# A graph layer's first stage: weights in one array, and layernorm chunks in a written order

## The chip, the core and the metric

The kernel runs on one core of a Trainium2 chip. The time is that of one execution on the device in microseconds (us); the median of several runs counts. A core has five engines that run side by side: PE (TensorE, matrix products), DVE (VectorE), ACT (ScalarE), POOL (GpSimd) and SP (SyncE, here only a sender of DMAs). Each takes its own instructions in order and waits for the others through semaphores. DMAs are sent from the queues of SP, ACT and POOL and are carried out by 16 shared DMA engines.

## What is computed

A graph network over 12,500 nodes of 64 values and 412,500 edges of 32 values, sorted by receiver:

```python
h = jnp.maximum(_layernorm(x, axis=-1), 0.0)
msg_in = concat(h[src], h[dst], edge_attr)
messages = swish(msg_in @ W1 + b1) @ W2 + b2
att = softmax(swish(msg_in @ Wa1 + ba1) @ Wa2 + ba2, axis=0)
aggregated = segment_sum(messages * att, dst, 12500)
out = x + swish(concat(h, aggregated) @ Wu1 + bu1) @ Wu2 + bu2
```

All of it is in 32-bit floats.

## The kernel before, in words

Nodes are padded to NB = 98 blocks of 128. Since `msg_in @ W` is a sum of a sender's, a receiver's and an edge's part, the kernel computes the first two once per node. The work has three stages.

**First stage** (lines 97 to 252). The weights are sent to SBUF by many small DMAs, 23 of the first DMAs on the ACT queue among them (with base_sb and the zeros behind tr_d), four on SP's. Some are laid out twice, so that one matrix product serves two blocks (`w_pair`, `we`), which needs memsets on DVE and several DMAs each; DVE then halves them, because swish is computed with tanh. x is read in seven chunks of 14 blocks (CB = 14), with three buffers `xc`. For each chunk DVE forms the mean (L208, L209), subtracts it (L211), ACT squares (L213), DVE sums the squares and scales (L215, L216), ACT takes the root (L217), DVE forms reciprocal and h (L218, L220). PE transposes h (L228), ACT copies the result to hT (L229), PE multiplies it by the sender weights (L234), ACT copies the product to ts (L236), and SP stores ts to ts_d in HBM (L237). Behind the chunks, ACT sends the store of hT (L238), DVE prepares the window numbers (`windows()`, L192 to L202), and a second loop makes the receivers' table: PE (L248), DVE adds the bias (L250), the ACT queue stores tr_d (L252), with two buffers `tr`.

The order of the instructions on each engine is set by a scheduler, from the dependences and its own costs, except where an instruction stands in `tc.keep_in_program_order` (named `pin` elsewhere): these keep the order in which they are written. In the first stage of the kernel before only the matmuls of the tr loop (L248) are so held.

**The loop over edges** (`one_pass`). For each of 403 groups of 1,024 edges POOL sends eight gathers (L373), each of 128 rows of ts_d by the indices in src_sb. There are eight buffers `gs`, so POOL may be eight groups ahead of those who read them. SP loads a window of tr_d, the edges' values and the receivers (`wins`, `eo`, `db`), PE multiplies (L400), DVE adds the gathered rows (L405), and ACT, DVE and PE work on the result. Before the loop DVE makes constants (L315 to L337), among them `wu2h`, loaded by two DMAs of the ACT queue (L326) and halved (L327). The memory of these constants and of `eo` and `db` is that of the first stage, set free when its last stores have landed.

**The update** at the end reads the sums and writes the output.

A DMA from SP or ACT takes one of eight semaphore lanes in turn. The instruction that sends it also waits for the DMA that had that lane eight transfers earlier.

Of the kernel before, what the change touches and what calls it, by code (L numbers as in the profile page):

```python
# [51 lines left out]
P = 128  # L52
# [18 lines left out]
BIG = 3.0e38  # L71
WHY = "a receiver's number; windows past the last node are padded"
# [3 lines left out]
def gnn_kernel(ctx: ExitStack, tc: tile.TileContext, n_edges, x, src, dst, dst_row, first, edge,  # L76
               W1, b1, W2, b2, Wa1, ba1, Wa2, ba2, Wu1, bu1, Wu2, bu2, out):
# [5 lines left out]
    CB = 14 if NB % 14 == 0 else 1  # L83
# [17 lines left out]
    w_pair = const.tile([P, 2, 2, C], F32, name="w_pair")  # L101
    nc.vector.memset(w_pair, 0.0)
    for r in range(2):
        for h, eng in ((0, nc.sync), (1, nc.scalar)):
            rows = slice(h * D, (h + 1) * D)
            eng.dma_start(w_pair[rows, r, h, 0:U], Wa1[r * D:(r + 1) * D, :])
            eng.dma_start(w_pair[rows, r, h, U:C], W1[r * D:(r + 1) * D, :])
    w_bu = const.tile([D + 1, U], F32, name="w_bu")
    nc.scalar.dma_start(w_bu[:D, :], Wu1[0:D, :])
    nc.scalar.dma_start(w_bu[D:D + 1, :], bu1[None, :])  # L110

    we = const.tile([P, C], F32, name="we")
    nc.vector.memset(we, 0.0)
    for r in (0, 64, 96):
        nc.scalar.dma_start(we[r:r + DE, 0:U], Wa1[2 * D:, :])
        nc.scalar.dma_start(we[r:r + DE, U:], W1[2 * D:, :])
    nc.vector.tensor_scalar(we, we, 0.5, None, op0=ALU.mult)
# [3 lines left out]
    nc.scalar.dma_start(base_sb[:, :NG], first)  # L121

    def across(ap, n, name, dtype=F32, parts=P):
        t = const.tile([parts, n], dtype, name=name)
        nc.scalar.dma_start(t, bass.AP(tensor=ap.tensor, offset=ap.offset, ap=[[0, parts], [1, n]]))
        return t

    bias = const.tile([P, C], F32, name="bias")
    for ap, c in ((ba1, 0), (b1, U)):
        nc.scalar.dma_start(bias[:, c:c + U],  # L130
                            bass.AP(tensor=ap.tensor, offset=ap.offset, ap=[[0, P], [1, U]]))
    wa2 = across(Wa2, U, "wa2")
    ba2_c = across(ba2, 1, "ba2_c")
    bu2_r = across(bu2, D, "bu2_r")
    w2b = const.tile([S1, U], F32, name="w2b")
    nc.scalar.dma_start(w2b[:U, :], W2)
    nc.scalar.dma_start(w2b[U:S1, :], b2[None, :])
    wu1a = const.tile([U, U], F32, name="wu1a")
    nc.scalar.dma_start(wu1a, Wu1[D:, :])
    wu2 = const.tile([U, D], F32, name="wu2")  # L140
    nc.scalar.dma_start(wu2, Wu2)
# [19 lines left out]
    nc.scalar.dma_start(tr_d[NP:, :], zero[:WR, :])  # L161
# [11 lines left out]
    with tc.tile_pool(name="node1", bufs=1) as node1, \  # L173
            tc.tile_pool(name="node", bufs=2) as node, \
            tc.tile_pool(name="node_ps", bufs=2, space=PSUM) as node_ps:
        x_v = x.rearrange("(p b) d -> p b d", b=NB)
        xcs = []
        for c in range(0, NB, CB):
            xc = node.tile([P, CB, D], F32, name="xc", bufs=3)
            nc.sync.dma_start(xc, x_v[:, c:c + CB, :])  # L180
            xcs.append(xc)
        nc.sync.dma_start(src_sb, src)
        dst_sb = node1.tile([P, T], I32, name="dst_sb")
        nc.sync.dma_start(dst_sb, dst)
        base_p = node1.tile([P, NG], I32, name="base_p")
        nc.sync.dma_start(base_p, bass.AP(tensor=first.tensor, offset=first.offset,
                                          ap=[[0, P], [1, NG]]))
        hT = node1.tile([2 * D, NB // 2, P], F32, name="hT")

        def windows():  # L190

            nc.vector.tensor_tensor(dloc.rearrange("p (g k) -> p g k", k=K),  # L192
                                    dst_sb.rearrange("p (g k) -> p g k", k=K),
                                    base_p[:, :, None].to_broadcast([P, NG, K]), ALU.subtract)
            last4 = dloc.rearrange("p (g k) -> p g k", k=K)[:, :, H:]
            nc.vector.tensor_scalar(last4, last4, -float(SHIFT), None, op0=ALU.add)
            for h in range(2):
                nc.vector.tensor_scalar(bj[:, :, h], base_p[:WR, :], iota_p[:WR], float(SHIFT * h),
                                        op0=ALU.add, op1=ALU.add)
            fall = node1.tile([P, NG - 1], F32, name="fall")  # L200
            nc.vector.tensor_tensor(fall, base_p[:, :NG - 1], base_p[:, 1:], ALU.subtract)
            nc.vector.tensor_reduce(far[:, 2:3], fall, AX.X, ALU.max)  # L202

        nc.vector.tensor_scalar(w_pair, w_pair, 0.5, None, op0=ALU.mult)
        for c in range(0, NB, CB):
            xc = xcs[c // CB]
            mean = node.tile([P, CB], F32, name="mean")
            nc.vector.tensor_reduce(mean, xc, AX.X, ALU.add)  # L208
            nc.vector.tensor_scalar(mean, mean, 1.0 / D, None, op0=ALU.mult)  # L209
            xm = node.tile([P, CB, D], F32, name="xm")  # L210
            nc.vector.tensor_tensor(xm, xc, mean[:, :, None].to_broadcast([P, CB, D]), ALU.subtract)  # L211
            sq = node.tile([P, CB, D], F32, name="sq")
            nc.scalar.activation(sq, xm, AF.Square)  # L213
            rstd = node.tile([P, CB], F32, name="rstd")
            nc.vector.tensor_reduce(rstd, sq, AX.X, ALU.add)  # L215
            nc.vector.tensor_scalar(rstd, rstd, 1.0 / D, EPS, op0=ALU.mult, op1=ALU.add)  # L216
            nc.scalar.activation(rstd, rstd, AF.Sqrt)  # L217
            nc.vector.reciprocal(rstd, rstd)  # L218
            h = node.tile([P, CB, D], F32, name="h")
            nc.vector.scalar_tensor_tensor(h, xm, 0.0, rstd[:, :, None].to_broadcast([P, CB, D]),  # L220
                                           op0=ALU.max, op1=ALU.mult)
            ts = node.tile([P, CB, C], F32, name="ts")
            for b in range(0, CB, 8):
                n = min(8, CB - b)
                q = (c + b) // 2
                pt = node_ps.tile([P, 4, P], F32, name="pt")
                for i in range(n // 2):
                    nc.tensor.transpose(pt[:, i, :], h[:, b + 2 * i:b + 2 * i + 2, :], ident)  # L228
                nc.scalar.copy(hT[:, q:q + n // 2, :], pt[:, :n // 2, :])  # L229
                for i in range(0, n, 4):  # L230
                    m = min(4, n - i)
                    pn = node_ps.tile([P, 4, C], F32, name="pn", bufs=3)
                    for k in range(0, m, 2):
                        nc.tensor.matmul(pn[:, k:k + 2, :], hT[:, q + (i + k) // 2, :], w_pair[:, 0],  # L234
                                         start=True, stop=True)
                    nc.scalar.copy(ts[:, b + i:b + i + m, :], pn[:, :m, :])  # L236
            nc.sync.dma_start(ts_d.rearrange("(p b) f -> p b f", b=NB)[:, c:c + CB, :], ts)  # L237
        nc.scalar.dma_start(hT_d, hT)  # L238
        nc.vector.tensor_scalar(bias, bias, 0.5, None, op0=ALU.mult)
        windows()  # L240
        for c in range(0, NB, CB):
            tr = node.tile([P, CB, C], F32, name="tr")
            for b in range(0, CB, 4):
                n = min(4, CB - b)
                pn = node_ps.tile([P, 4, C], F32, name="pn", bufs=3)
                for i in range(0, n, 2):
                    tc.keep_in_program_order(
                        nc.tensor.matmul(pn[:, i:i + 2, :], hT[:, (c + b + i) // 2, :], w_pair[:, 1],  # L248
                                         start=True, stop=True))
                nc.vector.tensor_tensor(tr[:, b:b + n, :], pn[:, :n, :],  # L250
                                        bias[:, None, :].to_broadcast([P, n, C]), ALU.add)
            nc.scalar.dma_start(tr_d[:NP, :].rearrange("(p b) f -> p b f", b=NB)[:, c:c + CB, :], tr)  # L252
# [40 lines left out]
def one_pass(tc, n_edges, v):  # L293
# [6 lines left out]
    wa2, ba2_c, w2b, wu1a, wu2, we, gather = (  # L300
        v[k] for k in ("wa2", "ba2_c", "w2b", "wu1a", "wu2", "we", "gather"))
# [8 lines left out]
    with ExitStack() as ctx:  # L310
# [11 lines left out]

        wu2h = keep.tile([P, 2, D], F32, name="wu2h")
        nc.vector.memset(wu2h, 0.0)
        for h in range(2):
            nc.scalar.dma_start(wu2h[h * U:(h + 1) * U, h, :], wu2)  # L326
        nc.vector.tensor_scalar(wu2h, wu2h, 0.5, None, op0=ALU.mult)  # L327
# [486 lines left out]

# [38 lines left out]
```

## Time and profile before

| what | us |
|---|---|
| median of 3 runs | 4180.05 (4179.7 to 4185.37) |
| profiled execution | 4179.44 |
| its span, first to last instruction | 4177.7 |

Work of the first stage, from the groups between 20 and 98 us by shape:

| line, engine | shape | count | mean ns |
|---|---|---|---|
| L213 ACT square | 128x896 | 7 | 948 |
| L229 ACT copy to hT | 128x512 | 7 | 586 |
| L236 ACT copy to ts | 128x512 | 21 | 586 |
| L211 DVE subtract | 128x896 | 5 | 1072 |
| L215 DVE sum of squares | 128x896 | 7 | 1080 |
| L220 DVE h | 128x896 | 7 | 1087 |
| L192 DVE window numbers | 128x3224 | 1 | 3501 |

The profile is read as follows. A group's row names the line, the engine, the operation and its tiles with their shapes, then the busy time and the mean of one instruction, and behind a bar the engine's idle time just before such instructions with what ended it. "issue" there is time in which the engine waited for nothing that the profile shows. A row of the waits has the total, the number and the longest. In the timeline each row has the start and the duration in us; "SPq" and "ACTq" rows are the sending of DMAs, not the transfers. Trace records name two PE instructions for each 128x256 matmul in 32-bit floats, so "x14" are the seven products of a chunk.

### The profile page before, as it was taken

To read this page: it belongs to the slowest core of one execution; us is meant where nothing else is said; L and a number is where in the kernel's file an instruction comes from. 1 tells how busy PE (TensorE), PEld (TensorE's weight loads), DVE (VectorE), ACT (ScalarE), POOL (GpSimd) and SP (SyncE) were. 2 spreads that over 40 slices of the span, in tenths; PEclk is the share of its full clock that TensorE was granted. 3 is DMA by queue.
4 is the path that set the end of the run, shared out by engine and by line. 5 is a ranking of instruction groups with operands and counts; after the bars stand their busy time and mean duration, and the time that the engine had idled before them with its cause. 6 is when DMAs were issued, how large, how long until landed. Compare 5 with 4: busy or idle time off the path is not lost.

```text
span 4177.7 us, 43813 instructions
## 1 busy us (share of the span) xinstructions
PE 2250.2 (54%) x10980; PEld 1686.0 (40%) x10980; DVE 2879.0 (69%) x7713; ACT 600.1 (14%) x1229; POOL 3048.7 (73%) x3236
## 2 busy tenths in 40 slices
PE   5644556445555555555555555555555555555555
PEld 4433344333334433444334443343444334434344
DVE  5766767666767766766666666676676666766668
ACT  3211111111111111111111111111111111111112
POOL 2777777777777777777777777777777777777772
PEclk9566666666666666656666566566565665666665
DMA  6433334333333333333333333333323333333323
GB/s 246 112 86 101 101 95 102 96 100 103 95 95 91 83 88 89 81 89 83 87 89 80 89 86 84 90 80 90 90 80 90 82 88 90 80 90 82 87 77 110
DMA packets 232283, 392.22 MB, mean 94 GB/s; under 512 B 99797, under 2 KB 158294, under 8 KB 218838
## 3 DMA queue, kind: packets, MB, share of 16 engines
q0 software_dynamic: 103168, 211.49, 19.0%
q1 hardware_dynamic: 125808, 167.82, 15.3%
q10 hardware_dynamic: 3046, 10.02, 0.6%
q8 instruction: 91, 1.49, 0.2%
q14 instruction: 170, 1.39, 0.1%
HBM read 363.29 MB, written 25.72 MB: 93 GB/s over the span
## 4 chain that ended last, share of the span: by engine, by line


## 5 line engine op out<-in xcount | busy, mean ns | idle before, releaser
L373 POOL DMA_INDIRECT gs<-ts_d,src_sb x3224 | 3047.1, 945 | 1055.2 <-issue 884.1
L400 PE MATMUL pe<-wins,eo 128*128 128x256 f32 x3224 | 1405.3, 612 | 1183.2 <-issue 1132.6
L400 PEld LDWEIGHTS pe<-wins,eo 128*128 128x128 f32 x3224 | 959.6, 312 | 1460.3 <-issue 1198.1
L405 DVE TENSOR_TENSOR gs<-pe,gs 128x1024 f32<-128x1024 f32 x403 | 492.0, 1221 | 1115.7 <-DMA gs<-ts_d,src_sb 1108.2
L406 ACT ACTIVATE pe<-gs 128x1024 f32<-128x1024 f32 x403 | 415.6, 1031 | 2777.4 <-DVE gs L405 2315.9
L468 DVE TENSOR_SCALAR wt<-iota_w,dloc,p 128x40 f32<-128x40 f32 x3224 | 726.1, 317 | 0.1
L474 PE MATMUL sp<-wt,acts 128*65 128x40 f32 x6448 | 586.0, 261 | 0.9 <-DVE wt L468 0.9
L474 PEld LDWEIGHTS sp<-wt,acts 128*65 128x65 f32 x6448 | 535.3, 173 | 27.0 <-DVE wt L468 1.0
L444 PE MATMUL mt<-ident,mx 128*128 128x128 f32 x103 | 48.4, 470 | 515.0 <-DVE sums L498 508.8
L416 DVE SCALAR_TENSOR_TENSOR acts<-pe,gs 128x512 f32<-128x512 f32 x403 | 272.0, 675 | 27.6 <-ACT pe L406 27.6
L424 DVE TENSOR_TENSOR pe<-pe,wa 128x512 f32<-128x512 f32 x403 | 281.6, 699 | 12.8
L422 DVE SCALAR_TENSOR_TENSOR pe<-pe,gs 128x512 f32<-128x512 f32 x403 | 280.6, 696 | 11.5 <-ACT pe L406 0.2
L427 DVE TENSOR_REDUCE lg<-pe 128x8 f32<-128x512 f32 x403 | 276.9, 687 | 10.4
L396 DVE TENSOR_SCALAR eo<-db,bj 64x256 f32<-64x256 int32 x806 | 274.1, 378 | 7.6
L485 PEld LDWEIGHTS mt<-ss,w2u 65*64 65x64 f32 x806 | 99.8, 175 | 396.4 <-issue 383.4
L485 PE MATMUL mt<-ss,w2u 65*64 65x40 f32 x806 | 150.8, 281 | 162.9 <-DVE gm L451 150.9
L444 PEld LDWEIGHTS mt<-ident,mx 128*128 128x128 f32 x103 | 18.6, 180 | 528.2 <-DVE sums L498 521.1
L455 ACT ACTIVATE scale<-fall 128x1 f32<-128x1 f32 x103 | 20.9, 203 | 514.2 <-DVE fall L454 514.2
L499 DVE COPY sums<-nmax 64x40 f32 x403 | 79.6, 198 | 9.1 <-issue 0.3
L480 ACT COPY ss<-sp 65x40 f32<-65x40 f32 x403 | 73.4, 182 | 25.5 <-PE sp L474 25.3
L498 DVE TENSOR_TENSOR sums<-sums,mt 64x40 f32 x300 | 53.5, 178 | 2.9 <-PE mt L485 1.6
L275 ACT COPY bu<-mt 64x512 f32<-64x512 f32 x24 | 25.8, 1076 | 150.1 <-PE mt L272 144.4
(96 smaller groups left out, 596.7 us busy)
## 6 DMA issues: line engine op xcount, KB each, us to landing
gs<-ts_d,src_sb POOLq DMA_INDIRECT x3224
eo<-in_edge_dram SPq DMA_DIRECT2D x100, 512.0 KB
db<-in_dst_row_dram SPq DMA_DIRECT2D x200, 256.0 KB
wins<-tr_d SPq DMA_DIRECT2D x806, 32.0 KB
ts_d<-ts SPq DMA_DIRECT2D x7, 896.0 KB
tr_d<-tr ACTq DMA_DIRECT2D x7, 896.0 KB
xc<-in_x_dram SPq DMA_DIRECT2D x7, 448.0 KB
hT_d<-hT ACTq DMA_DIRECT2D x1, 3136.0 KB
```

The lines of the kernel that those rows point to most:

```text
L373: nc.gpsimd.indirect_dma_start(out=gs[:, j, :], out_offset=None, in_=ts_d[:, :], in_offset=bass.IndirectOffsetOnAxis(ap=src_sb[:, t + j:t ...
L396: pin(nc.vector.tensor_scalar(eo[:WR, e], db[:, e], bj[:, g, h:h + 1], None, op0=ALU.is_equal))
L400: pin(nc.tensor.matmul(pe[:, 2 * q:2 * q + 2, :], eo[:, q * P:(q + 1) * P], win[:, q // 2, :, :], start=True, stop=True))
L405: pin(nc.vector.tensor_tensor(gss[g], pes[g], gss[g], ALU.add))
L406: pin(nc.scalar.activation(pes[g], gss[g], AF.Tanh))
L416: pin(nc.vector.scalar_tensor_tensor(acts[g % ACTS][:, :, 0:U], th[:, :, U:C], 1.0, gs[:, :, U:C], op0=ALU.add, op1=ALU.mult))
L422: pin(nc.vector.scalar_tensor_tensor(att, th[:, :, 0:U], 1.0, gs[:, :, 0:U], op0=ALU.add, op1=ALU.mult))
L424: pin(nc.vector.tensor_tensor(att, att, wa2[:, None, :].to_broadcast([P, K, U]), ALU.mult))
L427: pin(nc.vector.tensor_reduce(lgs[s][:, k:k + K], att, AX.X, ALU.add))
L468: pin(nc.vector.tensor_scalar(wt[:, j, :], iota_w[:, j // H, :], dloc[:, g * K + j:g * K + j + 1], p[:, k + j:k + j + 1], op0=ALU.is_equal ...
L474: pin(nc.tensor.matmul(sp, acts[g % ACTS][:, j, :], wt[:, j, :], start=j == 0, stop=j == K - 1))
L485: pin(nc.tensor.matmul(pp, w2u, sps.pop(g), start=True, stop=True))
```

## The change

All weights are laid out on the host in one array of 128 partitions by 1281 values, with zeros, doubled and repeated parts in place; two DMAs of the ACT queue bring it, and one DVE operation halves the first 896 columns (`w_pair`, `we`, `bias`, `wu2h`). x is read in eight chunks of 8, 14, 14, 14, 14, 14, 12 and 8 blocks with a buffer for each. The layernorm is split into `squares`, `deviation`, `normal` and `senders`, whose instructions are all held in the order written, which interleaves the chunks. The mean's scaling goes into the subtraction and the variance's scaling and eps into ACT's root. The transposes of a chunk all stand ahead of its products, and `pn` has four buffers. The load of base_sb goes to SP. The stores of the zeros and of hT, and windows(), stand behind the loop that makes tr.

```diff
-    CB = 14 if NB % 14 == 0 else 1
+    CB = 14 if NB % 14 == 0 else 2
...
-    w_pair = const.tile([P, 2, 2, C], F32, name="w_pair")
-    nc.vector.memset(w_pair, 0.0)
-    for r in range(2):
-        for h, eng in ((0, nc.sync), (1, nc.scalar)):
-            rows = slice(h * D, (h + 1) * D)
-            eng.dma_start(w_pair[rows, r, h, 0:U], Wa1[r * D:(r + 1) * D, :])
-            eng.dma_start(w_pair[rows, r, h, U:C], W1[r * D:(r + 1) * D, :])
...
+    nh = sum(n for _, n in PARTS[:HALVED])
+    nc.scalar.dma_start(w_all[:, :nh], weights[:, :nh])
+    nc.scalar.dma_start(w_all[:, nh:], weights[:, nh:])
...
-    nc.scalar.dma_start(tr_d[NP:, :], zero[:WR, :])
...
-        for c in range(0, NB, CB):
-            xc = node.tile([P, CB, D], F32, name="xc", bufs=3)
-            nc.sync.dma_start(xc, x_v[:, c:c + CB, :])
+        sizes = [8] + [min(CB, NB - 16 - c) for c in range(0, NB - 16, CB)] + [8] if NB > 16 else [NB]
+        chunks = [(sum(sizes[:i]), n) for i, n in enumerate(sizes)]
+        for c, n in chunks:
+            xc = node.tile([P, CB, D], F32, name="xc", bufs=min(len(chunks), 8))[:, :n, :]
+            nc.sync.dma_start(xc, x_v[:, c:c + n, :])
             xcs.append(xc)
         nc.sync.dma_start(src_sb, src)
+        nc.sync.dma_start(base_sb[:, :NG], first)
...
+        def squares(i):
+            n = chunks[i][1]
+            total = node.tile([P, CB], F32, name="total")[:, :n]
+            pin(nc.vector.tensor_reduce(total, xcs[i], AX.X, ALU.add))
+            xm = xms[i] = node.tile([P, CB, D], F32, name="xm", bufs=3)[:, :n, :]
+            pin(nc.vector.scalar_tensor_tensor(xm, total[:, :, None].to_broadcast([P, n, D]), -1.0 / D,
+                                               xcs[i], op0=ALU.mult, op1=ALU.add))
+            sq = sqs[i] = node.tile([P, CB, D], F32, name="sq", bufs=3)[:, :n, :]
+            pin(nc.scalar.activation(sq, xm, AF.Square))
+
+        def deviation(i):
+            n = chunks[i][1]
+            rstd = rstds[i] = node.tile([P, CB], F32, name="rstd")[:, :n]
+            pin(nc.vector.tensor_reduce(rstd, sqs.pop(i), AX.X, ALU.add))
+            pin(nc.scalar.activation(rstd, rstd, AF.Sqrt, bias=eps, scale=1.0 / D))
+
+        def normal(i):
+            n = chunks[i][1]
+            rstd = rstds.pop(i)
+            pin(nc.vector.reciprocal(rstd, rstd))
+            h = hs[i] = node.tile([P, CB, D], F32, name="h")[:, :n, :]
+            pin(nc.vector.scalar_tensor_tensor(h, xms.pop(i), 0.0,
+                                               rstd[:, :, None].to_broadcast([P, n, D]),
+                                               op0=ALU.max, op1=ALU.mult))
+
+        def senders(i):
+            c, nn = chunks[i]
+            h = hs.pop(i)
+            ts = node.tile([P, CB, C], F32, name="ts")[:, :nn, :]
+            pts = []
+            for b in range(0, nn, 8):
+                n = min(8, nn - b)
+                pt = node_ps.tile([P, 4, P], F32, name="pt")
+                for k in range(n // 2):
+                    pin(nc.tensor.transpose(pt[:, k, :], h[:, b + 2 * k:b + 2 * k + 2, :], ident))
...
+                pin(nc.scalar.copy(hT[:, q:q + n // 2, :], pt[:, :n // 2, :]))
+            for b in range(0, nn, 4):
+                m = min(4, nn - b)
+                pn = node_ps.tile([P, 4, C], F32, name="pn", bufs=4)
+                for k in range(0, m, 2):
+                    pin(nc.tensor.matmul(pn[:, k:k + 2, :], hT[:, (c + b + k) // 2, :],
+                                         w_pair[:, 0], start=True, stop=True))
+                pin(nc.scalar.copy(ts[:, b:b + m, :], pn[:, :m, :]))
+            pin(nc.sync.dma_start(ts_d.rearrange("(p b) f -> p b f", b=NB)[:, c:c + nn, :], ts))
...
-        nc.scalar.dma_start(hT_d, hT)
-        nc.vector.tensor_scalar(bias, bias, 0.5, None, op0=ALU.mult)
-        windows()
...
+        squares(0)
+        if len(chunks) > 1:
+            squares(1)
+        pin(nc.vector.tensor_scalar(w_all[:, :nh], w_all[:, :nh], 0.5, None, op0=ALU.mult))
+        for i in range(len(chunks)):
+            deviation(i)
+            if i:
+                senders(i - 1)
+            if i + 2 < len(chunks):
+                squares(i + 2)
+            normal(i)
+        senders(len(chunks) - 1)
+        for c, nn in chunks:
...
+            pin(nc.scalar.dma_start(
+                tr_d[:NP, :].rearrange("(p b) f -> p b f", b=NB)[:, c:c + nn, :], tr))
+        pin(nc.scalar.dma_start(tr_d[NP:, :], zero[:WR, :]))
+        pin(nc.scalar.dma_start(hT_d, hT))
         windows()
...
-        wu2h = keep.tile([P, 2, D], F32, name="wu2h")
-        nc.vector.memset(wu2h, 0.0)
-        for h in range(2):
-            nc.scalar.dma_start(wu2h[h * U:(h + 1) * U, h, :], wu2)
-        nc.vector.tensor_scalar(wu2h, wu2h, 0.5, None, op0=ALU.mult)
```

## The prediction

> **What bounds the kernel now.** I first read the page's busy shares and its groups. The chain of waits, which would come next, is empty for this profile, so the bound has to be found from the waits and the timeline.
>
> ```profile
> span 4177.7 us, 43813 instructions
> PE 2250.2 (54%) x10980; PEld 1686.0 (40%) x10980; DVE 2879.0 (69%) x7713; ACT 600.1 (14%) x1229; POOL 3048.7 (73%) x3236
> ...
> L373 POOL DMA_INDIRECT gs<-ts_d,src_sb x3224 | 3047.1, 945 | 1055.2 <-issue 884.1
> ...
> L405 DVE TENSOR_TENSOR gs<-pe,gs 128x1024 f32<-128x1024 f32 x403 | 492.0, 1221 | 1115.7 <-DMA gs<-ts_d,src_sb 1108.2
> ```
>
> POOL is busy 73% and DVE, the next, 69%. But POOL's idle time is nearly all "issue": time in which it waited for nothing. DVE's largest wait is the other way round, for the gathered rows. The view of POOL's own waits splits POOL's idle time:
>
> ```profile
> POOL gs L373 <- issue: 884.1, 2901, 0.3
> POOL gs L373 <- DMA tr_d<-tr: 72.9, 1, 72.9
> POOL gs L373 <- DMA gs<-ts_d,src_sb: 53.3, 175, 0.3
> POOL gs L373 <- DVE eo L396: 27.1, 89, 0.3
> ```
>
> Every one of these waits is 0.3 us, the normal distance between two gathers, but for one of 72.9 us ahead of the first. So POOL never stalls once it has begun. The tile view puts the first gather at 75.3 and the last at 4103.8: (4103.8 - 75.3) / 3223 = 1.250 us each. The span is then **75.35 (first stage) + 3224 x 1.250 (4029.4) + 73.0 (what follows the last gather)** = 4177.7. The change touches only the first term and, by what it hands on, perhaps the second.
>
> What ends the 72.9 us? The label names the store of tr, but the gather (L373) reads ts_d and src_sb, and the compiled order has it wait on the queue lanes of the seven ts stores and not on those of hT_d or tr. The timeline of the first stage (start, duration) shows how the last of them comes about:
>
> ```profile
> 20.30 0.55 ACTq L161 DMA_DIRECT2D tr_d<-zero  x1
> ...
> 20.88 1.28 ACT L213 ACT_TABLE_LOAD   x1 [20.88 <-DMA wu1a<-in_Wu_dram]
> ...
> 22.17 1.79 ACT L213 ACTIVATE sq<-xm 128x896 f32<-128x896 f32 x2
> ...
> 35.64 0.99 ACT L229 COPY hT<-pt 128x512 f32<-128x512 f32 x2
> 35.78 28.94 SPq L237 DMA_DIRECT2D ts_d<-ts  x7
> 36.30 2.89 PEld L234 LDWEIGHTS pn<-w_pair,hT 128*128 128x128 f32 x14 [1.04 <-ACT hT L229]
> 36.30 3.29 PE L234 MATMUL pn<-w_pair,hT 128*128 128x256 f32 x14 [0.81 <-ACT hT L229]
> ...
> 60.98 0.35 ACTq L238 DMA_DIRECT2D hT_d<-hT  x1
> ...
> 75.35 1.10 POOL L373 DMA_INDIRECT gs<-ts_d,src_sb  x1 [72.95 <-DMA tr_d<-tr]
> ```
>
> Three pieces: ACT does nothing until 20.88 because its queue is issuing 23 small DMAs, each waiting for an earlier one's lane; seven chunks then take until the last ts store at 64.4 (tile view), 6 us each; and that store needs 75.35 - 64.4 = 10.9 us to land, beside the 3136 KB of hT_d issued 3.4 us earlier.
>
> **The change, part by part.** All times are from the span's start; chunks are now 8, 14, 14, 14, 14, 14, 12, 8 blocks.
>
> *Weights (2 DMAs in place of 21 on ACT and 4 on SP; base_sb goes to SP, the zeros go last).* ACT is free at about 2 us (two issues of 0.6 from 0.82); its table load of 1.28 needs no data. Five DVE operations on weights go here (memsets, halvings), two more in the loop's preparation; one halving of 128x896 comes, by L204's 0.43 for 512 elements some 0.7 us. SP sends x at once instead of after its four weight pieces. The bytes grow to 655 KB (zeros included); x (3.2 MB), weights, src and dst (1.6 MB each) are 7.3 MB, at the 292 to 366 GB/s of the rows 12 to 28 us some 22 us, but x goes first: a 448 KB chunk takes 1.5 us at that rate and is needed every 5.6 us. Hidden, except for the first two chunks: in before the first landed at 4.31; I take 4.0 for the first (256 KB) and 6.5 for the second.
>
> *The first chunk.* DVE: sum and centre chunk 0 (0.69 each, as L427 and L416 for 512 elements): 5.4; chunk 1 (1.08 twice) 6.5 to 8.7; halving 9.4; variance sum 0: 10.1; chunk 2: 12.3; reciprocal 0.2 and h 0.68: 13.2; variance sum 1: 14.3. ACT: squares 0 and 1 until 9.7, second table load until 11.0, sqrt 0, square 2 until 13.3, sqrt 1 (it waits for DVE) until 14.6. Only then, in the written order, the copies of chunk 0: hT 0.6, four matmuls at 0.72 (the first chunk's pace in before, 5.07 us for seven; 3.29 later) and the last copy: 18.6. Square 3 and sqrt 2: **19.85**. Removed means, scale and eps operations (0.17 each) are DVE work that is not on this path.
>
> *A chunk in the steady order.* DVE per 14 blocks: 4 x 1.08 + 0.23 = 4.55 us. ACT's written order is sqrt, two hT copies, four ts copies, square of two chunks on, next sqrt. From the trace of before, hT copy to first matmul is 35.64 to 36.30 = 0.66, the last ts copy ends 3.75 after the first matmul; square 0.95, sqrt 0.22, handoffs 0.05: 0.66 + 3.75 + 0.95 + 0.22 + 0.05 = **5.63**. That exceeds DVE's 4.55, so the ACT-PE ring paces. In before, hT copies came at 35.64, 40.06, 45.95, 51.19, 55.58: 4.4 to 5.9 apart, so pinning by itself gains little; it is the late start that goes.
> From 19.85: chunks 1 and 2, 5.63 each: 31.1; chunk 3 (12-block square 0.83): 36.6; chunk 4 (8-block square 0.57): 41.85; chunk 5 with only sqrt: 46.5; chunk 6, three full copies, 0.66 + 1.17 + 2 x 0.86 + 0.59 = 4.14: 50.6; chunk 7: 0.66 + 1.17 + 0.86 + 0.59 = 3.28: **53.9**.
> Here a rule bears: the Trainium skill, TensorE: Matmul & The Clock Gate, Part 1, says the array runs at half clock until it has been busy for a window of about 3.4 us, and again after an idle one. The rows by stretch (length, busy time and count of each engine, then granted clock, DMA share, GB/s):
>
> ```profile
> 72.00:76.00 4.00, 0.55 (x3) 0.14 (x1) 0.46 (x1) 0.00 (x0) 0.65 (x1) 1.00 1.01 418
> 76.00:80.00 4.00, 3.72 (x11) 2.90 (x12) 2.48 (x6) 0.00 (x0) 3.09 (x4) 0.71 0.70 275
> ```
>
> After a PE gap of 3.74 us inside these rows the clock fell to 0.71; but before's matmuls kept their 3.29 us a chunk after gaps of 0.4 to 1.7 us. The new ring leaves PE gaps of about 1.3 us, so I charge the slow pace once (1.0 us, in the sum). Were gaps of that kind to keep it cold, 1.8 us a chunk for six would add 10.7 and the gain would be 7.
>
> *The last store.* 512 KB, and hT_d and tr_d's tail of zeros no longer go ahead of it. Bounds: 10.9 us as now; the nearest clean row is the last tr store, issued at 93.0 (tile view) and landed at 97.27, 4.3 us for 896 KB; less 384 KB at the 382 GB/s of that stretch (1.0 us) is **3.3**. I take 3.3, since the 10.9 fits the bytes: 3.2 MB of hT_d and two stores of 0.9 MB from 61 to 75 us are 5 MB in 14 us, at the 361 to 470 GB/s these rows show. Against small transfers stands the Trainium skill, DMA: Bandwidth & Descriptors, section Bandwidth, that transfers below 1 MiB waste the rate[...]. In before ACT's ts copies never waited for a store 4.4 to 6.6 us old, so the extra store is not on the path; I charge nothing for it. First gather: 53.9 + 0.1 + 3.3 = **57.3**.
>
> *What is handed on.* hT_d now goes behind all tr stores. DVE's preparation of the loop (L315 on) and SP's loop loads reuse that memory, so they now wait for hT_d's landing. Bytes after 54 us: tr 6.4 MB and hT 3.2 MB; in before the rows of 64 to 96 us average 340 GB/s, with up to 52 for gathers in it (64 KB each 1.25 us); at 290 net that is 33 us, and 2 to land: about 89, against 97.27. From there to the first addition of gathered rows (L405) before took until 111.03, 13.8 us, set by the loads of wins (PE waited 14.9 for them), so the 4.6 us wait on wu2h that goes was beside them; about 103. POOL may run eight groups ahead (8 buffers x 10 us): until 57.3 + 80 = 137. The first group is done some 5 us after its addition, at 108: **29 us of cover**, so POOL doesn't stall. Then DVE needs about 6 us a group against POOL's 10 and catches up as it did before. Moving windows() (6 us on DVE) behind the tr stage, base_sb to SP (one issue of 0.3) and wu2h out of the loop's preparation cost nothing under that cover. The 73.0 us at the end stay.
>
> **Sum**: 75.35 - 57.3 = 18.0 us less. The profiled execution is 4179.44 (span 4177.7 and 1.7 around it), the median 4180.05, 0.6 apart, so 4180.05 - 18 = **4162**. An uncertain step is worth its own microseconds and nothing is multiplied; changes under 0.2% (8.4 us) can't be told from none.
>
> **Rivals.**
> 1. *The ring overlaps better*, and PE alone paces at 4.41 (before's last three chunks): 18.6 + 5 x 4.41 + 4.14 + 3.28 + 3.4 = 51.5, gain 24: 4156. For it: hT copies 4.4 apart in before. Against: there no square stood between them, in the new order one does.
> 2. *The last store lands no faster*, since tr stores still start as it goes: 53.9 + 10.9 = 64.8, gain 10.5: 4169.5. Against: tr's first store has only 512 KB and comes later.
> 3. *It doesn't do what it says*: PE stays cold, or ts stores wait behind the src and dst loads: gain under 8.4; 4173.
> 4. *Slower*: hT_d last holds the loop's start so long that the eight buffers run out. It decides only once hT_d lands after about 118 us (89 + 29), and then costs a microsecond for each; to be slower by 8.4 it would have to land after 144, at a mean rate of 109 GB/s. Rates of 183 to 382 with gathers running speak against it. 4189.
>
> **Chances.** Forecast 0.72 (4156.5 to 4168), rival 1 0.10, rival 2 0.11, rival 3 0.05, rival 4 0.02. Faster: 0.93; same: 0.05; slower: 0.02. The range, 4153 to 4170, takes in rivals 1 and 2.
>
> **What would show it.** First gather at 57 (51 to 65); 3224 gathers still 1.250 apart with no wait over 0.4; hT copies of the 14-block chunks 5.6 apart; first square near 5.5; last ts store issued near 54 and 3 to 4 us from the gather; the loop's first memset near 89 and L405's first near 103. Wrong if a gather waits for DVE or ACT, or the chunk pace is that of DVE or loads.

## The result, and the profile after

The changed kernel takes 4167.01 us (median of 7 runs, 4165.77 to 4167.37), the kernel before 4180.05 (7 runs, 4179.4 to 4185.37). The ratio is 0.9966, its 95% interval 0.9954 to 0.9977: 13.0 us less, where 18.0 were forecast. The forecast's ratio, 0.9957, lies in that interval too; that the gain was smaller is read from the runs, none of which is under 4165.77, and from the traces. The profiled execution of the changed kernel took 4166.68 us, 1.8 more than its span. First the page: span, busy shares, and the rows of the gather and of the addition of gathered rows (now L382 and L414).

```profile
span 4164.9 us, 43769 instructions
...
PE 2237.8 (54%) x10980; PEld 1678.3 (40%) x10980; DVE 2873.2 (69%) x7698; ACT 600.9 (14%) x1230; POOL 3052.8 (73%) x3236
...
L382 POOL DMA_INDIRECT gs<-ts_d,src_sb x3224 | 3051.2, 946 | 1038.3 <-issue 930.2
...
L414 DVE TENSOR_TENSOR gs<-pe,gs 128x1024 f32<-128x1024 f32 x403 | 491.8, 1220 | 1116.6 <-DMA gs<-ts_d,src_sb 1103.8
```

Hardly anything shows here, for the change moves some tens of microseconds out of four thousand. One number is new: the gathers are busy 3051.2 us and not 3047.1. The view of POOL's own waits shows the other sign (total, number, longest):

```profile
POOL gs L382 <- issue: 930.2, 2876, 54.0
POOL gs L382 <- DMA gs<-ts_d,src_sb: 60.8, 193, 1.7
```

The 54.0 is the wait ahead of the first gather, 72.9 before. But the second row's longest was 0.3 before and is 1.7 now: POOL does stall after it has begun. The timeline of the first stage (start, duration, engine, and in brackets the idle time before) shows the part that went as meant:

```profile
1.75 1.28 ACT L203 ACT_TABLE_LOAD   x1 [1.75 <-PEq L878]
6.26 0.63 ACT L203 ACTIVATE sq<-xm 128x512 f32<-128x512 f32 x1 [3.23 <-DVE xm L200]
...
20.14 0.95 ACT L231 COPY hT<-pt 128x512 f32<-128x512 f32 x2
...
25.45 0.96 ACT L231 COPY hT<-pt 128x512 f32<-128x512 f32 x2
...
52.16 0.58 ACT L238 COPY ts<-pn 128x512 f32<-128x512 f32 x1 [0.23 <-PE pn L236]
52.77 0.32 SPq L239 DMA_DIRECT2D ts_d<-ts  x1
...
56.44 1.10 POOL L382 DMA_INDIRECT gs<-ts_d,src_sb  x1 [54.04 <-issue]
```

ACT begins at 1.75 in place of 20.88, chunks follow 5.3 us apart, the last ts store goes at 52.77, and the first gather starts 3.67 later, at 56.44: **18.9 us sooner** than the 75.35 of before. So the first stage gave more than the kernel gained. The last gather starts at 4090.97; (4090.97 - 56.44) / 3223 = 1.2518 us from one to the next, where before had 1.2499 by the same count. Times 3223 that is **6.1 us lost**. From the start of the last gather to the end both take 73.9. 18.9 - 6.1 = 12.8, the difference of the two spans.

Where do the 6.1 go? POOL's timeline, early in its run:

```profile
76.58 0.94 POOL L382 DMA_INDIRECT gs<-ts_d,src_sb  x1 [0.30 <-issue]
77.83 3.36 POOL L382 DMA_INDIRECT gs<-ts_d,src_sb  x1 [0.30 <-issue]
81.49 1.32 POOL L382 DMA_INDIRECT gs<-ts_d,src_sb  x1 [0.30 <-issue]
...
91.86 0.94 POOL L382 DMA_INDIRECT gs<-ts_d,src_sb  x1 [0.30 <-issue]
93.20 0.94 POOL L382 DMA_INDIRECT gs<-ts_d,src_sb  x1 [0.40 <-DMA gs<-ts_d,src_sb]
95.82 0.94 POOL L382 DMA_INDIRECT gs<-ts_d,src_sb  x1 [1.67 <-DMA gs<-ts_d,src_sb]
97.38 0.94 POOL L382 DMA_INDIRECT gs<-ts_d,src_sb  x1 [0.62 <-DMA gs<-ts_d,src_sb]
98.85 0.94 POOL L382 DMA_INDIRECT gs<-ts_d,src_sb  x1 [0.53 <-DMA gs<-ts_d,src_sb]
```

Two things, both where before had gathers of 0.94 us and waits of 0.3. Two gathers are themselves long, by 2.42 and 0.38 us: 2.8. And four wait for the rows of earlier gathers, 0.1 + 1.37 + 0.32 + 0.23 = 2.0 above the usual 0.30. That leaves 1.3 us spread over the rest of the loop, which is no more than that rest differs between kernels: counted against 1.25 us a gather, the gathers after 104 us lost from -1.0 to +0.9 us in the traces of before, this kernel and the four that follow. DVE's timeline over the same stretch:

```profile
76.86 3.50 DVE L178 TENSOR_TENSOR dloc<-dst_sb,base_p 128x3224 f32<-128x3224 int32 x1
...
80.98 1.03 DVE L182 TENSOR_SCALAR dloc<-dloc 128x1612 f32<-128x1612 f32 x1
...
91.00 0.06 DVE L330 MEMSET nmax<- 128x1 f32 x1 [7.23 <-DMA hT_d<-hT]
...
105.02 1.23 DVE L414 TENSOR_TENSOR gs<-pe,gs 128x1024 f32<-128x1024 f32 x1 [8.15 <-PE pe L409]
```

The long gathers lie beside the two long operations of windows(). In before these ran ahead of all gathers:

```profile
34.38 3.50 DVE L192 TENSOR_TENSOR dloc<-dst_sb,base_p 128x3224 f32<-128x3224 int32 x1
...
40.87 0.99 DVE L196 TENSOR_SCALAR dloc<-dloc 128x1612 f32<-128x1612 f32 x1
```

The 3.36 us gather starts 0.97 after the DVE operation and ends at 81.19, 0.83 after that ends at 80.36; the second ends at 82.81, 0.80 after its DVE operation. That is nearly a whole gather (0.94) after DVE is done: as if POOL had stood still in between. The waits for rows come just as the large store of hT, issued at 78.0, has landed (91.0) and the loop's first loads go out.

### The profile page after: what moved, and what is told of

Read it like the earlier page. It is cut to its first block, busy times and chain, and to the rows that moved or that the text cites. A ratio compares the mean times of both kernels' runs of the same rounds, so it can differ in the third digit from the quotient of the medians.

```text
span 4164.9 us, 43769 instructions
## 1 busy us (share of the span) xinstructions
PE 2237.8 (54%) x10980; PEld 1678.3 (40%) x10980; DVE 2873.2 (69%) x7698; ACT 600.9 (14%) x1230; POOL 3052.8 (73%) x3236
## 4 chain that ended last, share of the span: by engine, by line
## 5 line engine op out<-in xcount | busy, mean ns | idle before, releaser
L382 POOL DMA_INDIRECT gs<-ts_d,src_sb x3224 | 3051.2, 946 | 1038.3 <-issue 930.2
L414 DVE TENSOR_TENSOR gs<-pe,gs 128x1024 f32<-128x1024 f32 x403 | 491.8, 1220 | 1116.6 <-DMA gs<-ts_d,src_sb 1103.8
L425 DVE SCALAR_TENSOR_TENSOR acts<-pe,gs 128x512 f32<-128x512 f32 x403 | 271.9, 675 | 27.7 <-ACT pe L415 27.6
L433 DVE TENSOR_TENSOR pe<-pe,w_all 128x512 f32<-128x512 f32 x403 | 281.4, 698 | 12.8
L431 DVE SCALAR_TENSOR_TENSOR pe<-pe,gs 128x512 f32<-128x512 f32 x403 | 280.4, 696 | 11.2
```

Of the source, the lines that this page charges most:

```text
L382: nc.gpsimd.indirect_dma_start(out=gs[:, j, :], out_offset=None, in_=ts_d[:, :], in_offset=bass.IndirectOffsetOnAxis(ap=src_sb[:, t + j:t ...
L414: pin(nc.vector.tensor_tensor(gss[g], pes[g], gss[g], ALU.add))
L425: pin(nc.vector.scalar_tensor_tensor(acts[g % ACTS][:, :, 0:U], th[:, :, U:C], 1.0, gs[:, :, U:C], op0=ALU.add, op1=ALU.mult))
L431: pin(nc.vector.scalar_tensor_tensor(att, th[:, :, 0:U], 1.0, gs[:, :, 0:U], op0=ALU.add, op1=ALU.mult))
L433: pin(nc.vector.tensor_tensor(att, att, wa2[:, None, :].to_broadcast([P, K, U]), ALU.mult))
```

## The experiments

Two theories of the lost 6 us. **DVE holds POOL** (PORT in the expectations): windows() beside gathers lengthens them, and moving it ahead of the first gather brings the time back. **The store delays the rows** (STORE): hT's 3.2 MB beside the loop's first loads hold up the gathered rows, and moving the store brings it back. A rival to both: it is only the loop's jitter, and neither edit does anything. The first three kernels are the other corners of a square: each edit alone, and both. On the chip where these ran the kernel before took 4179.99 us, 0.06 less than beside the changed kernel, which was not run again there.

**windows() before the tr loop**

```diff
         senders(len(chunks) - 1)
+        windows()
...
         pin(nc.scalar.dma_start(hT_d, hT))
-        windows()
```

> The changed kernel with windows() between the senders of the last chunk and the tr loop, where DVE waits 6.4 us for PE. Theory PORT (DVE's window operations, 3.5 and 1.0 us long on SBUF, hold up POOL while it makes the gathers beside them): the two long gathers at 77.8 and 81.5 us (3.36 and 1.32 us for 0.94) go, 2.8 us; the waits for gathered rows at 92 to 99 us (2.0 us) stay: median about 4164.2. Theory STORE (the store of hT_d, in flight from 78 to 91 us, holds up both): all 4.8 us stay, 4167. First gather at 56.4 in both.

Measured: 4162.91 us (4161.99 to 4164.91, 5 runs), ratio to before 0.9959 [0.9945, 0.9973]. First gather 56.91. No gather is over 1.2 us; the waits for rows between 89 and 100 us stay (five, up to 1.20). The first gather comes 0.5 later than in the changed kernel, but not by DVE's six microseconds ahead of the tr loop: DVE got the first chunk of x at 5.22 and not at 4.82, and already the first ts store went 0.5 later (19.7 against 19.2). POOL's tile view and its wait for rows:

```profile
L382 POOL DMA_INDIRECT gs<-ts_d,src_sb x3224: 938/944/1189, 56.9 to 4088.0; - x190
```

```profile
POOL gs L382 <- DMA gs<-ts_d,src_sb: 28.3, 84, 1.2
```

**hT stored in pieces, behind each chunk's ts store**

```diff
             pin(nc.sync.dma_start(ts_d...[:, c:c + nn, :], ts))
+            pin(nc.scalar.dma_start(hT_d[:, c // 2:(c + nn) // 2, :], hT[:, c // 2:(c + nn) // 2, :]))
...
-        pin(nc.scalar.dma_start(hT_d, hT))
```

> The changed kernel with the store of hT cut into eight pieces, each on the ACT queue just behind its chunk's ts store, so that nothing of it is left when the gathers run; windows() stays at the end. PORT: a gather of about 3.4 us stays beside the 3.5 us window operation, the waits of 2.0 us at 92 to 99 go: about 4165. STORE: both go, about 4162. If the pieces delay the last ts store, the first gather comes later than 56.4 by as much.

Measured: 4165.24 us (4162.79 to 4166.15), 0.9963 [0.9949, 0.9977]. First gather 56.95. The stalls at 93 to 99 are gone (the first row below is that of the waits), while a long gather stays. Its timeline, with DVE and POOL together:

```profile
POOL gs L382 <- DMA gs<-ts_d,src_sb: 20.7, 68, 0.3
```

```profile
77.37 3.51 DVE L178 TENSOR_TENSOR dloc<-dst_sb,base_p 128x3224 f32<-128x3224 int32 x1
...
78.33 4.08 POOL L382 DMA_INDIRECT gs<-ts_d,src_sb  x1 [0.30 <-issue]
...
81.31 0.98 DVE L182 TENSOR_SCALAR dloc<-dloc 128x1612 f32<-128x1612 f32 x1
```

Here one gather spans both: 78.33 to 82.41, until 0.12 after the end of the second DVE operation. The last piece of hT went out at 52.7, so its store isn't what lengthens this gather.

**Both edits**

> Both edits: hT in pieces and windows() ahead of the tr loop. PORT and STORE agree here: no gather over 1.3 us and no wait over 0.4 in the first 150 us, gathers 1.250 apart from the first on, about 4161.5. If it stays near 4167, the loss is spread over the loop and belongs to neither.

Measured: **4161.18 us** (4160.59 to 4161.97), 0.9954 [0.9938, 0.9971]: 5.8 us under the changed kernel and faster than both kernels of this case. Its tile view of the gathered rows (duration least/median/most in ns, first and last start) and its timeline:

```profile
L382 POOL DMA_INDIRECT gs<-ts_d,src_sb x3224: 940/945/1187, 57.1 to 4086.3; - x190
```

```profile
81.63 0.06 DVE L330 MEMSET nmax<- 128x1 f32 x1 [4.11 <-DMA tr_d<-tr]
...
94.52 1.22 DVE L414 TENSOR_TENSOR gs<-pe,gs 128x1024 f32<-128x1024 f32 x1 [3.46 <-PE pe L409]
```

In before the same row was:

```profile
L373 POOL DMA_INDIRECT gs<-ts_d,src_sb x3224: 940/944/1193, 75.3 to 4103.8; - x190
```

The longest of 3224 gathers is 1.19 us in both, and the pace is (4086.3 - 57.14) / 3223 = 1.2501: the old one. The loop's start moves forward too, by 9.4 and 10.5 us (81.63 from 91.00, 94.52 from 105.02), which buys nothing by itself, since POOL had no lack of buffers.

The square adds up. windows() early is worth 4167.01 - 4162.91 = 4.1 us with the one store and 4165.24 - 4161.18 = 4.1 with the pieces; the pieces are worth 1.8 and 1.7. The 4.1 exceed the 2.8 of the two long gathers, and the 3.1 of the one with the pieces (4.08 for 0.94), by about a microsecond, no more than the rest of the loop differs between these kernels. So each theory holds for its half: windows() makes the long gathers, the late store the waits for rows. The rival of mere jitter falls: the runs of the kernel with both edits lie wholly under those of each of the others. This rests on the single runs and on the traces; the intervals of the ratios to before overlap, and so do the runs of the changed kernel and of the pieces alone (4165.77 to 4167.37 and 4162.79 to 4166.15).

**The store of hT at the front again** (with the rest of the change kept) tests the step that gave the last ts store 3.3 us in place of 10.9.

```diff
         senders(len(chunks) - 1)
+        pin(nc.scalar.dma_start(hT_d, hT))
...
-        pin(nc.scalar.dma_start(hT_d, hT))
```

> The changed kernel with the whole store of hT sent right behind the last ts copy, ahead of the tr stores, as in the kernel before. If the 10.9 us of before's last ts store were the bytes of hT_d beside it (the prediction's step), the store takes 8 to 11 us again in place of 3.6, the first gather comes at 61 to 64, the 2.0 us of waits go, and the time is 4170 to 4173. If the landing had another cause (rival 2's reading), the first gather stays at 56.4 and the time is about 4165.

Measured: 4171.54 us (4169.62 to 4173.25, 17 runs), 0.998 [0.9972, 0.9987]. Its tile view, the gather and the ts stores:

```profile
L382 POOL DMA_INDIRECT gs<-ts_d,src_sb x3224: 940/944/3178, 63.5 to 4094.0; - x190
L239 SPq DMA_DIRECT2D ts_d<-ts x8: 319/320/327, 18.8 to 52.4; - x8
```

The last ts store goes at 52.4, no later than in the changed kernel, but the first gather starts 11.1 us after it instead of 3.67. By the first gather, a store of 512 KB thus takes three times as long to land with 3.2 MB issued 0.6 us ahead of it. The long gather (3.18 us, beside L178) stays and the waits for rows are gone, which is the third place of the store (with the pieces, and both edits) that has none.

**What gave the 18.9 us?** The next six take the change apart. They ran on other chips, on which the kernel before itself takes 5461 to 5463 us: there the gathers begin at the same distance of 1.25 us, but the rest of the loop is slow. So their times are given, and only the first stage is read from them; instructions last as long there (0.58 us a ts copy), but an offset between the chips of some tenths isn't excluded. "Weights alone" is the kernel before with the new weight array and its two DMAs, and base_sb on SP. The two parts that follow are put into it, or taken from the change:

```diff
# weights alone, hT last / before, hT last
-        nc.scalar.dma_start(hT_d, hT)
...
             # end of the tr loop
+        tc.keep_in_program_order(nc.scalar.dma_start(hT_d, hT))
# weights alone, hT in pieces on SP (the ts stores are held in order too)
-        nc.scalar.dma_start(hT_d, hT)
...
+            keep(nc.sync.dma_start(hT_d[:, c // 2:(c + CB) // 2, :], hT[:, c // 2:(c + CB) // 2, :]))
# change, order left to the compiler
+        pin = lambda i: i
# change, equal chunks
+        sizes = [CB] * (NB // CB)
```

> The kernel before with only the weights in one array and two DMAs (base_sb moved to SP with it); seven chunks of 14, hT_d and windows() where they were, order by the scheduler. If the late start of ACT (20.9 us) was the main loss: first square near 8, the seven chunks at the old pace of 6.2 us, last store as slow as before (11 us): first gather 12 to 14 us earlier than 75.35, time 4166 to 4168, gathers undisturbed at 1.250. If the loads of x were what the first stage waited for, under 6 us are gained: above 4174.

> The kernel before with only the store of hT_d moved behind the tr stores; windows() stays early. The last ts store then lands in about 4.3 us in place of 10.9: first gather near 69, 6.5 us earlier. Theory PORT: gathers disturbed only by the store's share of 2.0: gain 4.5, 4175.5. Theory STORE: 4.8 us are lost again, gain under 2: 4178 to 4179.

> The changed kernel with the first stage's instructions left to the scheduler instead of held in the written order (the tr loop's too). The compiled order then puts the store of hT_d ahead of the last ts copies, the zeros first, and windows() among the last chunks. Theory ORDER (the written order is worth something by the stores it puts last, and nothing by its interleaving): ring pace 5.3 within 0.4 a chunk, last ts store slow again, first gather 61 to 65, no disturbed gathers: 4168 to 4172. Rival (the interleaving itself paces): chunks over 6 us apart, first gather after 66, over 4173.

> The changed kernel with seven chunks of 14 blocks. The small first chunk lets ACT begin about 1.5 us earlier and the small last one takes 1.1 us off the last copies and 1.0 off the last store, against one more chunk's handoff of 1 us: first gather at 57.5 to 60, time 4168 to 4170.5. If chunk size is worth nothing: 4167.

> The kernel before with two parts of the change only: weights in one array, and the store of hT_d behind the tr stores. Chunks are seven of 14 in the scheduler's order, windows() early. If the parts add (62.2 for the weights alone, 7.1 for the store alone), the first gather comes at 55.1, 1.3 earlier than in the changed kernel, so that written order and chunk sizes cost 1.3. Then 2 to 3.3 us of gather waits beside hT_d's store: about 4163 where the kernel before takes 4180. If the written order is needed for the gain, the first gather is at 57 or later.

> The same with hT stored in seven pieces by SP, each right behind its chunk's ts store, so that nothing of it meets the gathers. First gather at 55 to 56, no gather over 1.5 us apart early on, 4159.5 to 4161 where the kernel before takes 4180: a little better than both. If pieces crowd the ts stores, the first gather is at 57 or later and the time 4161 to 4163.

| kernel | time, us (before there) | ratio to before [95%] | last ts store | first gather | between |
|---|---|---|---|---|---|
| before (the chip of the result) | 4180.05 | | 64.4 | 75.35 | 11.0 |
| changed kernel (the chip of the result) | 4167.01 | 0.9966 [0.9954, 0.9977] | 52.77 | 56.44 | 3.67 |
| before, hT last | 5464.71 (5460.71) | 1.0006 [0.9992, 1.0019] | 63.6 | 68.25 | 4.7 |
| weights alone | 5448.41 (5460.71) | 0.9970 [0.9955, 0.9985] | 51.2 | 62.18 | 11.0 |
| change, order left to the compiler | 5445.31 (5460.71) | 0.9984 [0.9970, 0.9997] | 52.4 | 62.19 | 9.8 |
| change, equal chunks | 5456.41 (5460.71) | 0.9994 [0.9982, 1.0005] | 51.4 | 55.98 | 4.6 |
| weights alone, hT last | 5456.46 (5463.24) | 0.9989 [0.9974, 1.0004] | 52.4 | 56.97 | 4.6 |
| weights alone, hT in pieces | 5458.67 (5463.24) | 0.9984 [0.9970, 0.9997] | 51.6 | 55.98 | 4.4 |

The ratio is the one on record, not the quotient of the medians. The last three columns can be read off the tile view of each kernel; for "before, hT last" and for "weights alone", in this order, the gather and the ts stores are:

```profile
L373 POOL DMA_INDIRECT gs<-ts_d,src_sb x3224: 938/944/1192, 68.2 to 5327.0; - x190
L237 SPq DMA_DIRECT2D ts_d<-ts x7: 319/320/327, 35.0 to 63.6; - x7
```

```profile
L348 POOL DMA_INDIRECT gs<-ts_d,src_sb x3224: 938/944/1189, 62.2 to 5334.4; - x190
L219 SPq DMA_DIRECT2D ts_d<-ts x7: 319/320/377, 22.3 to 51.2; - x7
```

The first leaves the stores late and shortens only the landing; the second leaves the landing and brings the stores 13.2 us forward. Together (weights alone, hT last) they give 75.35 - 56.97 = 18.4 of the change's 18.9. Simple addition, 13.2 + 7.1 = 20.3, had been expected and is missed by 1.9. The traces show where: 0.8 of the 7.1 came from a last store that went earlier (63.6 against 64.4) and not from its landing. And the products of the first chunk took longer, in "weights alone" and in "weights alone, hT last":

```profile
17.49 3.97 PE L216 MATMUL pn<-w_all,hT 128*128 128x256 f32 x14
```

```profile
17.25 5.49 PE L216 MATMUL pn<-w_all,hT 128*128 128x256 f32 x14
```

Their records start 0.43 us apart until 18.9 in the first and until 21.7 in the second, then 0.21 apart, and every later chunk follows 1.2 later in the second. In both traces the record of the granted clock begins, at full clock, at that very moment (18.90 and 21.75; there is no earlier record). It is another moment in each kernel here, so first gathers that differ by a microsecond are not told apart. Of the 13.2, too, 1.1 is this (5.07 us in before against 3.97).

The written order and the small chunks, the larger part of the diff, are then worth nothing that these runs can show; with hT in pieces on SP, without either, the first gather is at 55.98, as expected (55 to 56), and no gather is over 1.19 us. Left to the compiler, the order puts hT's store ahead of the last ts stores and so loses what the last place gave; its first gather (62.19) is near that of the pinned order with hT in front (63.46). With seven equal chunks the first gather comes at 55.98, where a later one was expected: a miss. The small last chunk does land sooner (3.67 against 4.6), as forecast from its bytes, but with an eighth chunk the last store goes 1.4 us later, part of which may again be PE's slow pace.

That kernel also repeats the main finding on another chip, since windows() stands behind the tr loop in it as in the change. Its timeline:

```profile
129.45 3.51 DVE L178 TENSOR_TENSOR dloc<-dst_sb,base_p 128x3224 f32<-128x3224 int32 x1
```

```profile
129.93 4.17 POOL L382 DMA_INDIRECT gs<-ts_d,src_sb  x1 [0.31 <-issue]
```

**Which property of the DVE operation holds POOL?** Two kernels put one more DVE operation of 3.5 us behind the tr loop of the best version: one with two inputs from SBUF, one with a single input. Its result is not used.

```diff
         pin(nc.scalar.dma_start(tr_d[NP:, :], zero[:WR, :]))
+        spare = node1.tile([P, T], F32, name="spare")
+        pin(nc.vector.tensor_tensor(spare, dst_sb, dst_sb, ALU.subtract))
# the other kernel
+        spare = node1.tile([P, 1], F32, name="spare")
+        pin(nc.vector.tensor_reduce(spare, dloc, AX.X, ALU.add))
```

> The kernel with both edits (hT in pieces, windows() early) and one operation added on DVE behind the tr loop, a subtraction of 128x3224 values with both inputs in SBUF, some 3.5 us; its result is not used. PORT: a gather that starts beside it takes as long as it, 3 us or more for 0.94, and the gathers lose 2 to 3.5 us once. Rival (any long DVE operation, or the transfers of these microseconds, hold gathers up): the same here, so the next run tells.

> The same with the added operation replaced by a sum over 128x3224 values, one input in SBUF, also some 3.4 us, at the same place. PORT: the gathers beside it keep 0.94 to 1.0 us and lose under 0.3. Rival: they lose 2 to 3.5 us as with two inputs.

Measured: 5456.81 us, 0.9982 [0.9964, 1.0], and 5453.68, 0.9987 [0.9975, 0.9999]. Both tell nothing on this question, for on those chips the tr loop ended so late that POOL had stopped for lack of buffers. In the kernel with two inputs DVE's operation, then POOL's gathers:

```profile
144.00 3.51 DVE L269 TENSOR_TENSOR spare<-dst_sb 128x3224 f32<-128x3224 int32 x1
```

```profile
135.81 0.94 POOL L384 DMA_INDIRECT gs<-ts_d,src_sb  x1 [0.30 <-issue]
164.51 0.94 POOL L384 DMA_INDIRECT gs<-ts_d,src_sb  x1 [27.76 <-issue]
```

No gather runs at 144. But the changed kernel's own trace holds the comparison, later in the loop: DVE reduces the same tile dloc, with one input and in the same 3.5 us. DVE's timeline there, then POOL's:

```profile
392.92 3.49 DVE L576 TENSOR_REDUCE far<-dloc 128x1 f32<-128x3224 f32 x1
```

```profile
393.08 0.94 POOL L382 DMA_INDIRECT gs<-ts_d,src_sb  x1 [0.30 <-issue]
394.33 0.95 POOL L382 DMA_INDIRECT gs<-ts_d,src_sb  x1 [0.30 <-DMA gs<-ts_d,src_sb]
395.58 0.94 POOL L382 DMA_INDIRECT gs<-ts_d,src_sb  x1 [0.30 <-issue]
```

Three gathers lie within that operation, all of the usual length. So a long DVE operation as such doesn't hold POOL; the subtraction of two tiles in SBUF (L178) does, in four kernels of four that ran it beside gathers, and beside the one-input scalar operation L182 a gather took 1.32 for 0.94. Nor do two inputs alone: counted over this trace, 962 gathers start while DVE runs an operation with one input in SBUF and one in PSUM, the memory of PE's results (L414, L425, L431, L433), and none of them took over 0.953. L178 also has integers as both its inputs, a difference that no run here takes away. This is what a rule says that the prediction should have weighed: the Trainium skill, SBUF — State Buffer, section Who interferes with whom, has DVE and GpSimd share a pair of ports, which one of them holds for its whole instruction; a DVE operation with two SBUF inputs contends with a GpSimd instruction that reads SBUF, a scalar operation can in its two-port modes, and a reduction on this chip never. The gather reads its indices (src_sb) from SBUF. An estimate by that rule for the gather at 77.83 is the 2.53 us that L178 still ran, and its own 0.94: 3.47, where 3.36 was measured. L178 began beside a gather already running, which kept its 0.94, and took 3.50 us itself, as it does without gathers (3.50 in before). The runs show the pattern; the port itself they do not show.

## Why the prediction held, and where it did not

The time lies inside the range, at the slow end of the forecast's own 4156.5 to 4168. The range had been made wide for other errors than the one that came, so it is partly luck that the number held.

*The bound* (one gather after another from 75.35 on, each microsecond of the first stage worth one): right; the end is still 73.9 us after the start of the last gather.

*Weights in two DMAs*: right. The queue of small DMAs ahead of ACT's first operation is gone, and the weight array alone gives 13.2 us, 1.1 of them by PE's pace. The first square came at 6.26 against 5.5, since DVE got the first chunk of x at 4.82 and not at 4.0; the second chunk's hT copy at 20.14 against 19.85.

*The ring of ACT and PE*: right in kind, a little dear. Chunks came 5.31, 5.33, 5.21, 5.00, 4.48 and 4.01 us apart against 5.63, 5.63, 5.5, 5.25, 4.65 and 4.1; last copy 52.74 against 53.9. Rival 1 (PE alone, 4.41) is out. The slow pace of the products, charged once, occurred once: the first chunk's four took 3.78 us, later seven 3.29, so the short gaps of PE did not bring it back.

*The last store*: right, 3.67 us against 3.3, and the reason given (bytes of hT ahead of it) is shown by hT at the front, 11.1, and by the kernel before with hT last, 4.7 in place of 11.0. Rival 2 is out. First gather 56.44 against 57.3.

*What is handed on*: the size of the wait was right (hT landed 91.0 against 89, first addition 105.02 against 103), and nothing waited for it: rival 4 didn't happen in the changed kernel. But this part holds the step that failed. It said "Moving windows() (6 us on DVE) behind the tr stage ... cost nothing under that cover", and the sum kept the gathers 1.250 apart. The cover was one of buffers: it shows that no gather waits for DVE's result. It says nothing of a gather held while DVE works. That term was zero and measured 4.1 us. The same holds for the store of hT, moved to where gathers run: counted as bytes ahead of the loop's start, not for what it does to gathers beside it, 1.7 to 1.8. Together they are 5.8; less the 0.9 by which the first gather came earlier than forecast, that is the distance from the forecast gain of 18.0 to the measured 13.0. The mark named in advance, 3224 gathers at 1.250 with no wait over 0.4, is the one that failed.

*Left open*: which property of L178 holds POOL, two inputs in SBUF or their type; and which transfer delays the rows at 93 to 99, since hT has landed by then and the loop's loads, which go out at 92, are also there without stalls when hT was stored sooner.

## What to carry to other kernels

Work that is moved out of the stage before the bound is free only if the bounding engine doesn't feel it while it runs: look not just at who waits for its result, but at which engine and which transfers it runs beside. When one engine's queue of equal instructions sets the time, read their number, distance and longest member; these three tell an early start from a slower pace. And before writing out an order by hand, try the one transfer and the one queue of small loads that the timeline shows to be late: here those two gave 18.4 of 18.9 us.

## What the hardware showed unexpectedly

A gather of 0.94 us took 3.18 to 4.17 us in four kernels beside one DVE subtraction of 3.5 us with two inputs in SBUF, on both kinds of chip, and 0.94 to 0.95 beside a reduction of the same length. PE's first products ran at half their later pace until a moment that differs from kernel to kernel (18.9 and 21.7 us in two that send the same work).

The same kernels take some 30% longer on some chips (before 4180 and 5461 us). In the kernel with two inputs the gathers still start 1.25 us apart at first, but from 89 us on DVE's additions of the tr loop come 11 us apart beside them, and POOL stops at 136.8, after (135.81 - 56.86) / 1.25 + 1 = 64 gathers, eight groups of eight: just the cover of eight buffers that the prediction counted (until 137). The mean granted clock is 0.60 there and 0.635 in the changed kernel, 6% and not 30; why those chips run the rest so slowly is not known from these runs.
